# A fourth profile of widths for the experts, and a hand-ordered opening and end for the attention between them

## The chip, the cores and the metric

The program runs on one core of a Trainium2 chip. The metric is the time of one execution in microseconds (us); the median of the three runs before is 4838.47 us (4837.74 to 4840.27). The core has a matrix engine (TensorE, PE in the profile, with its weight loads apart as PEld), VectorE (DVE), ScalarE (ACT), GpSimd (POOL) and SyncE (SP), which issues most of the DMAs. PSUM, where PE leaves its results, has eight banks of 512 f32 numbers for each of 128 partitions.

## What is computed

A block of a transformer on x, 8 batches of 1024 rows of 512 numbers, all in f32:

```
x = x + 0.5 * ffn(layernorm(x))      # mixture of 32 experts, one for each row
x = x + attention(layernorm(x))      # 16 heads of 32, rope, softmax over 1024 keys
x = x + 0.5 * ffn(layernorm(x))      # the same ffn weights again

def ffn(xt):                         # xt: 8192 rows
    probs  = softmax(xt @ w_router)
    top1   = argmax(probs);  gate = probs[top1]
    pos    = place of the row among the rows of its expert
    accepted = pos < C               # C = ceil(1.25 * 8192 / 32) = 320
    y      = (silu(buf @ w_gate) * (buf @ w_up)) @ w_down     # for each expert, its rows in buf
    return xt + where(accepted, y * gate, 0)
```

The ffn adds its own (normalised) input as well. How many rows an expert gets depends on the data: the reference's routing of the given inputs sends between 191 and 343 rows to an expert in the first ffn, and between 160 and 429 in the second.

## The kernel before

Four stages follow each other in one program: the router of the first ffn (`Block.front`), its experts (`Block.experts`), the attention (`Attention.run`), which also does the router of the second ffn on its way, and the experts of the second ffn.

**Experts.** `Block.sorted` ranks the 32 experts by their number of rows. `Block.experts` then holds one program for each entry of `profiles` (L67): entry i gives a width for every rank, and the first entry whose widths hold all the experts' rows (the more-than-width flags are counted on VectorE, L478 to L481) is run through a switch. An expert of width w is given w columns: 64 MATMUL records of w columns against 128x128 weights for gate and up (`gated`, L704; each f32 product is two records), then for each block of 128 rows the down product (`feed`, L745, and L753 for the third block, which only widths over 256 have), with the transposes of the next expert's rows between (L692). Weights come by DMA two experts ahead.

**Attention.** A unit (b, c) is four heads of one batch. `stage` (L886) runs 16 slots over a unit: the score products for the row maxima and sums of one unit ("tops": L1220 on PE, L1235 on VectorE, L1239 on ScalarE), the score products, exponentials and weighted sums of the unit before ("sums": L1200, L1227, L1232, L1302), and between them one group of other PE work out of `fill`: projections of q and k for the unit after (`project`, L1125), of v (L1170), or the output product of the batch before (`output`, L1328). Small tasks (`prepare`: rows of the next batch loaded, normalised, transposed; `rotated`: rope on a projection; `finished`: router and routing of finished rows) are generators that `step` and `product` advance by due times and a credit of VectorE time. On PE, ScalarE, VectorE and GpSimd the order in which the program is written is kept; the DMA issues of SP are ordered by the framework. A projection's rope takes eight small DMAs (L1147, L1148), a product on GpSimd (L1150) and two on VectorE (L1153, L1154); all projections, transposes and output products use one PSUM bank, tag "m".

**The opening.** `constants` (L1006) loads tables and biases, then the output weights, and works out the output bias (bv times Wo, plus bo) with four products (L1040), split into three bf16 pieces. `run` (L921) then loads the v weights, prepares the first half of batch 0 and the second half after it (rows loaded, measured, normalised and evicted on VectorE), loads the q and k weights, and runs the four projections q, k, k, q of unit (0, 0); then the first stage starts.

**The end.** After the last unit, a stage of sums alone has the four output products of the last batch's first half in its slots 9 to 12; the four of the second half follow with VectorE adding each to the rows loaded from `x1` and storing to `x2`. `finished` then takes the first half (rows read back from `x2`, the rest of the row put out, normalised, transposed, router, routing), and after that the second half in the same way; `ranked` ranks the experts, and the table of rows is written to HBM for the second `experts`.

Of the kernel before, what the change touches and what calls it, by code (L numbers as in the profile page):

```python
# [50 lines left out]
class Block:  # L51


    def __init__(self, nc, tc, T, D, E, F):
# [11 lines left out]
        C, q = self.C, P // 4  # L66
        self.profiles = [  # L67
            [C] * 10 + [C - q] * 9 + [C - 2 * q] * 8 + [C - 3 * q] * (E - 27),
# [131 lines left out]
    def logits(self, hs, lg, pool, psum, tag, bufs=2):  # L200
# [4 lines left out]
        for h in hs:  # L205
            if isinstance(h, tuple):
                yield h
                continue
            yield PE, 0.6
            self.transposed(psum, tag, xT[:, :, j * P : (j + 1) * P], h)  # L210
            j += 1
# [558 lines left out]
class Attention:  # L770
# [13 lines left out]
    def __init__(  # L784
# [15 lines left out]
        self.credit = 0.0  # L800
        self.hT, self.w_qk, self.qk, self.v, self.oT = ({} for _ in range(5))
        self.mrow, self.over, self.mv, self.held = ({} for _ in range(4))
# [110 lines left out]
    def run(self):  # L913
        nc, tc = self.nc, self.tc
        F, KD = mybir.EngineType, self.KD
        with (
# [6 lines left out]
            with tc.manual_schedule(engines={F.PE, F.Activation, F.DVE, F.Pool}):  # L923
                self.s.copy = nc.vector.tensor_copy
                self.load(2)
                for half in range(2):
                    self.start(self.prepare(0, half, 0))
                    self.finish()
                self.load_qk(0, 0)
                for f in self.project(0, 0):  # L930
                    at_once(f())
                    self.now += 1
                    self.step(100)
                self.finish()
                units = [(b, c) for b in range(self.B) for c in range(KD)]
                for i, (b, c) in enumerate(units):
                    self.stage(
                        (b, c), units[i - 1] if i else None, self.fill(b, c), self.begin(b, c),
                        whole=(i == 0),
                    )  # L940
# [6 lines left out]
                for f in self.output(b, 1):  # L947
                    at_once(f())
                    self.now += 1
                    self.step(100)  # L950
# [24 lines left out]
    def fill(self, b, c):  # L975

        qk = self.project(*self.following(b, c))
        if b == c == 0:
            self.v_groups = self.values(0)
            v, self.v_groups = self.v_groups[:7], self.v_groups[7:]  # L980
            return dict(enumerate(qk + v))
# [24 lines left out]
    def constants(self, wp):  # L1006
        nc, s, KD, L = self.nc, self.s, self.KD, self.L
        D = s.D
        bq, bk, bv, bo = self.biases

        self.cs, self.sn = (a.rearrange("p k c -> p (k c)")[:, 0:L] for a in s.acts)
        nc.sync.dma_start(self.cs, self.cos)
        nc.sync.dma_start(self.sn, self.sin)
# [18 lines left out]

        bo_ = self.pool.tile([P, D], F32, tag="oT", bufs=9, name="bo")
        nc.sync.dma_start(bo_, bo.partition_broadcast(P))
        self.load(3)
        pb = self.psum.tile([P, D], F32, tag="m", name="pb")
        for k in range(KD):
            wide = self.pool.tile([P, P], F32, tag="wide", name="wide")
            nc.vector.tensor_copy(wide, self.bias[:, 2, k : k + 1].to_broadcast([P, P]))
            nc.tensor.matmul(  # L1040
                pb, wide, self.w_vo[:, k, :], start=(k == 0), stop=(k == KD - 1)
            )
        nc.vector.tensor_tensor(bo_, bo_, pb, ALU.add)

        self.bo16 = wp.tile([P, D], BF16, name="bo16")
        nc.vector.memset(self.bo16, 0.0)
        piece = self.pool.tile([P, D], BF16, tag="piece", bufs=1, name="piece")
        for i in range(3):
            nc.vector.tensor_copy(piece, bo_)
            p = slice(i * 32, i * 32 + 1)  # L1050
            nc.vector.tensor_copy(self.bo16[p, :], piece[p, :])
            nc.vector.tensor_tensor(bo_, bo_, piece, ALU.subtract)

# [6 lines left out]
    def loaded(self, which):  # L1060

        self.load(which)
        yield from ()
# [3 lines left out]
    def prepare(self, b, half, later):  # L1067
# [26 lines left out]
        self.there.add((b, half))  # L1094

# [216 lines left out]
    def output(self, b, half):  # L1312
        nc, pool, KD, D = self.nc, self.pool, self.KD, self.s.D
        work = []
        for j in range(4):

            def group(j=j):
# [3 lines left out]
                x = pool.tile([P, D], F32, tag="xr", name="xr")  # L1321
                nc.sync.dma_start(x, self.x1[t * P : (t + 1) * P, :])
                acc = self.psum.tile([P, D], F32, tag="m", name="px")
# [23 lines left out]
    def finished(self, b, half, counted=None):  # L1347

        nc, s, pool, D = self.nc, self.s, self.pool, self.s.D
# [148 lines left out]
```

## Time and profile before

| | us |
|---|---|
| median of 3 runs | 4838.47 |
| the profiled execution: its time | 4848.97 |
| its span, first to last instruction | 4847.2 |
| first expert product of stage 1 to its last | 186.39 to 964.94 |
| first expert product of stage 2 to its last | 4057.87 to 4836.04 |
| first score product of the attention | 1032.54 |
| last weighted sum of the attention | 3962.9 |

All times below are from the start of the span. A line of a timeline has the start, the duration, the engine, the line of the code, the operation, what it writes and reads, the shapes and how many records are merged (x8); in brackets, how long the engine was idle before and who released it. In the table by stretches, each engine has its busy time and its records; PEclk is the share of full clock that was granted to PE, and the DMA share is the mean over 16 engines. The chain is followed backwards from the last instruction, each step to what released it.

### The profile page before, as it was taken

What the parts mean: (1) busy time and instruction counts of PE and PEld (TensorE: products, weight loads), DVE (VectorE), ACT (ScalarE), POOL (GpSimd) and SP (SyncE); (2) the same over time, 40 slices, a digit from 0 to 9 for tenths busy, and PEclk for the clock granted to TensorE, in tenths of its full rate; (3) what the DMA queues carried; (4) which work ended last, traced back from release to release, by engine and by line L of the source; (5) the groups of instructions that cost most, each with busy time, mean ns of one, the idle gap of its engine ahead of it and who ended that gap; (6) DMA issues with size and microseconds to landing.
All of it is one profiled execution on the core that took longest, in us unless ns stands there. A gap on an engine that the chain in (4) does not pass through costs nothing.

```text
span 4847.2 us, 68820 instructions
## 1 busy us (share of the span) xinstructions
PE 4596.5 (95%) x24572; PEld 2128.0 (44%) x24572; DVE 2836.3 (59%) x5568; ACT 2923.5 (60%) x5856; POOL 790.4 (16%) x787
## 2 busy tenths in 40 slices
PE   6699999968999999999999999999999886999999
PEld 4466667722233333333333333333333234666677
DVE  8433333356666767767777767767767744333332
ACT  6221212128998888888888888888888841111111
POOL 4433333210000010110110110110110002222221
PEclk8799999979999999999999999999999997999999
DMA  4455566521111212212212212212212124455554
GB/s 142 148 187 184 190 197 220 178 85 29 34 30 60 75 38 65 70 42 65 70 42 65 70 42 65 69 42 66 60 43 57 49 70 154 158 174 177 171 193 137
DMA packets 290581, 486.02 MB, mean 100 GB/s; under 512 B 47895, under 2 KB 83169, under 8 KB 290224
## 3 DMA queue, kind: packets, MB, share of 16 engines
q1 hardware_dynamic: 255376, 404.36, 26.8%
q0 software_dynamic: 34560, 76.93, 5.2%
q8 instruction: 196, 3.21, 0.3%
q14 instruction: 161, 1.32, 0.1%
q10 hardware_dynamic: 288, 0.20, 0.0%
HBM read 380.11 MB, written 89.72 MB: 97 GB/s over the span
## 4 chain that ended last, share of the span: by engine, by line
PE 82%; DVE 7%; ACT 4%; issue 3%; DMA 2%; POOL 1%; SPq 1%; another core or an unknown queue 0%; DVEq 0%; POOLq 0%; ACTq 0%
PE sa L1220 13%; PE gp L704 10%; PE up L704 9%; PE pq L1125 9%; PE po L1302 9%; PE yp L745 9%; PE sb L1200 6%; PE px L1328 4%; PE pv L1170 4%; PE sb L1227 3%; ACT junk L1239 2%; DVE nm L1235 2%; PE tp L194 2%; DMA table<-row,slot 1%; PE yp L753 1%
## 5 line engine op out<-in xcount | busy, mean ns | idle before, releaser
L1235 DVE TENSOR_REDUCE nm<-sa 128x2 f32<-128x1024 f32 x1024 | 1248.7, 1220 | 648.3 <-PE sa L1220 386.9
L1239 ACT ACTIVATE junk<-sa,nm 128x512 f32<-128x512 f32 x2048 | 1407.3, 687 | 257.6 <-DVE nm L1235 177.0
L1220 PE MATMUL sa<-k,q 32*128 32x512 f32 x4096 | 1149.1, 645 | 17.9 <-ACT junk L1239 11.1
L1232 ACT ACTIVATE pr<-sb 128x1024 f32<-128x1024 f32 x1024 | 1040.5, 1018 | 101.3 <-PE sb L1227 97.4
L1227 PE MATMUL sb<-q,k 32*128 32x512 f32 x4096 | 1062.1, 602 | 0.0
L709 ACT ACTIVATE sg<-gp 128x320 f32<-128x320 f32 (+3 forms) x256 | 102.6, 401 | 1166.2 <-PE gp L704 1164.2
L1150 POOL TENSOR_TENSOR raw<-raw,a 128x512 f32<-128x512 f32 x128 | 164.2, 1283 | 2401.7 <-DMA rot<-raw 1645.0
L1302 PE MATMUL po<-pr,v 128*32 128x512 f32 x4096 | 548.0, 606 | 0.1
L704 PE MATMUL gp<-bT,wg 128*128 128x320 f32 (+3 forms) x2048 | 530.7, 402 | 0.0
L704 PE MATMUL up<-bT,wu 128*128 128x320 f32 (+3 forms) x2048 | 524.8, 399 | 0.0
L1125 PE MATMUL pq<-hT,wqk 128*128 128x512 f32 x1024 | 511.3, 624 | 4.9 <-DVE raw L1140 3.9
L745 PE MATMUL yp<-wd,a 128*128 128x512 f32 x1024 | 460.3, 592 | 0.0
L704 PEld LDWEIGHTS gp<-bT,wg 128*128 128x128 f32 x2048 | 386.7, 190 | 115.7 <-issue 26.7
L1200 PE MATMUL sb<-mrow,ones 3*128 3x512 bf16 x2048 | 392.9, 384 | 42.0 <-ACT pr L1232 40.7
L728 DVE TENSOR_TENSOR a<-sg,up 128x320 f32<-128x320 f32 (+3 forms) x256 | 114.0, 445 | 541.6 <-PE up L704 371.1
L704 PEld LDWEIGHTS up<-bT,wu 128*128 128x128 f32 x2048 | 388.9, 190 | 94.1
L1200 PEld LDWEIGHTS <-ones 3*128 3x128 bf16 x2048 | 99.6, 91 | 709.6 <-issue 670.1
L1239 ACT ACTIVATION_READ_ACCUMULATOR junk<-sa,nm 128x1 f32 x2048 | 398.2, 194 | 0.0
L1227 PEld LDWEIGHTS sb<-q,k 32*128 32x128 f32 x4096 | 359.7, 184 | 0.1
L1220 PEld LDWEIGHTS sa<-k,q 32*128 32x128 f32 x4096 | 304.9, 184 | 81.3 <-ACT pr L1232 30.3
L1125 PEld LDWEIGHTS pq<-hT,wqk 128*128 128x128 f32 x1024 | 176.2, 191 | 323.8 <-issue 227.0
L749 DVE SCALAR_TENSOR_TENSOR ys<-yp,gates,x 128x512 f32<-128x512 f32 x128 | 96.1, 751 | 336.8 <-PE yp L745 336.8
(178 smaller groups left out, 4241.8 us busy)
## 6 DMA issues: line engine op xcount, KB each, us to landing
wg<-in_w_gate SPq DMA_DIRECT2D x64, 1024.0 KB
wu<-in_w_up SPq DMA_DIRECT2D x64, 1024.0 KB
wd<-in_w_down SPq DMA_DIRECT2D x64, 1024.0 KB
rot<-raw SPq DMA_DIRECT2D x1024, 32.0 KB
all<-in_x SPq DMA_DIRECT2D x32, 512.0 KB
xt<-first_rows SPq DMA_DIRECT2D x64, 256.0 KB
xr<-first_rows SPq DMA_DIRECT2D x64, 256.0 KB
d<-inverse SPq DMA_DIRECT2D x256, 64.0 KB
```

Of the source, the lines that this page charges most:

```text
L704: nc.tensor.matmul(acc, w[:, k, f * P : (f + 1) * P], to.bT[:, k, 0:width], start=(k == 0), stop=(k == s.KD - 1),)
L745: nc.tensor.matmul(yp, a[:, f, i * P : (i + 1) * P], wd[:, f, :], start=(f == 0), stop=(f == KF - 1),)
L1125: nc.tensor.matmul(acc, w[:, which, k, :], self.hT[b, n][:, k, :], start=(k == 0), stop=(k == KD - 1),)
L1170: nc.tensor.matmul(acc, hT[:, k, at : at + P], self.w_vo[:, k, :], start=(k == 0), stop=(k == KD - 1),)
L1200: nc.tensor.matmul(sb[:, h, :], self.ones16[at : at + 3, :], row[at : at + 3, :], start=True, stop=False,)
L1220: nc.tensor.matmul(sa[:, h, :], qa[at, (g * 4 + j) * P : (g * 4 + j + 1) * P], ka[at, m * 512 : (m + 1) * 512], start=True, stop=True,)
L1227: nc.tensor.matmul(sb[:, h, :], k[at, t * P : (t + 1) * P], q[at, n * 512 : (n + 1) * 512], start=False, stop=True,)
L1232: nc.scalar.activation(pr, sb, AF.Exp)
L1235: nc.vector.tensor_reduce(nm[:, m, j, pair : pair + 2], sa, AX.X, ALU.max, negate=True)
L1239: nc.scalar.activation(self.junk, sa[:, h - pair, :], AF.Exp, bias=nm[:, m, j, h : h + 1], accum_out=se[:, m, j, h : h + 1],)
L1302: nc.tensor.matmul(self.po[at : at + HD, :], self.v[b][t][:, c * P + at : c * P + at + HD], prs[h // 2 * 2][:, h % 2, :], start=(t == 0), ...
L1328: nc.tensor.matmul(acc, self.oT[b, c, half][:, j * P : (j + 1) * P], self.w_vo[:, c, :], start=False, stop=(c == KD - 1),)
```

## The change

- `profiles` gets a fourth entry, put first, with widths in steps of 16: 6 experts of 320, 1 of 304, 5 of 288, 6 of 272, 3 of 256, 5 of 240, 3 of 224, 3 of 208. Entry 0 before (10 of 320, 9 of 288, 8 of 256, 5 of 224) becomes entry 1.
- A new `opening` takes the place of the prologue in `run`. The q and k weights are loaded first, then the first four row tiles, the rope tables, and the other four row tiles (each half with buffers of its own). Each row tile is measured by itself; ScalarE normalises; three PSUM tags (s0 to s2, those of the scores) take the transposes; VectorE evicts the first half, ScalarE the second. Only k and q of the first half are projected before the first stage, the second half's transposes stand behind them, and the other two projections become the first two fills of that stage, in front of the eleven that it has.
- The output bias is worked out later: in stage (1, 1), with the first load of the output weights, and on one partition.
- At the end, the rows of the last batch stay on chip: they are not read back from `x2`. The second half's output products have the tags s0 to s2, and between them two turns of the first half's router work. ScalarE normalises and evicts the transposes of both halves; the second half's transposes use s0, s1, s2 and "po". The second half's router waits for the first half's logits, and only the routing waits for the first half's routing. The rest of the second half's rows is put out after the routing.

```diff
-        C, q = self.C, P // 4
+        C, q, h = self.C, P // 4, P // 8
         self.profiles = [
+            [C] * 6 + [C - h] + [C - 2 * h] * 5 + [C - 3 * h] * 6 + [C - 4 * h] * 3
+            + [C - 5 * h] * 5 + [C - 6 * h] * 3 + [C - 7 * h] * (E - 29),
             [C] * 10 + [C - q] * 9 + [C - 2 * q] * 8 + [C - 3 * q] * (E - 27),
...
-                self.load(2)
-                for half in range(2):
-                    self.start(self.prepare(0, half, 0))
-                    self.finish()
-                self.load_qk(0, 0)
-                for f in self.project(0, 0):
-                    at_once(f())
-                    self.now += 1
-                    self.step(100)
-                self.finish()
+                later = self.opening()
...
                 for f in self.output(b, 1):
                     at_once(f())
                     self.now += 1
-                    self.step(100)
+                    for _ in range(2):
+                        self.step(100)
+                        self.product()
...
-            return dict(enumerate(qk + v))
+            return dict(enumerate(ahead + qk + v))
...
     def loaded(self, which):
         self.load(which)
-        yield from ()
+        if which == 3 and not self.biased:
+            self.biased = True
+            yield from self.output_bias()
+
+    def output_bias(self):
+        nc, pool, KD, D = self.nc, self.pool, self.KD, self.s.D
+        bo = pool.tile([P, D], F32, tag="xr", name="bo")[0:1, :]
+        nc.sync.dma_start(bo, self.biases[3].partition_broadcast(1))
+        yield WAIT, 2
+        yield PE, 3.4
+        pb = self.psum.tile([P, D], F32, tag="m", name="pb")[0:1, :]
+        for k in range(KD):
+            nc.tensor.matmul(
+                pb, self.bias[:, 2, k : k + 1], self.w_vo[:, k, :],
+                start=(k == 0), stop=(k == KD - 1),
+            )
+        nc.vector.tensor_tensor(bo, bo, pb, ALU.add)
+        piece = pool.tile([P, D], BF16, tag="piece", bufs=1, name="piece")[0:1, :]
+        for i in range(3):
+            nc.vector.tensor_copy(piece, bo)
+            nc.vector.tensor_copy(self.bo16[i * 32 : i * 32 + 1, :], piece)
+            if i < 2:
+                nc.vector.tensor_tensor(bo, bo, piece, ALU.subtract)
...
+    def opening(self):
+        self.load_qk(0, 0)
...
+        xs = [fetch(0)]
+        nc.sync.dma_start(self.cs, self.cos)
+        nc.sync.dma_start(self.sn, self.sin)
+        xs.append(fetch(1))
...
+        for j in range(4):
+            measure(0, j)
+        for j in range(4):
+            measure(1, j)
+            kept(0, j, turn(0, j))
+        at_once(steps[-1])
+        self.there |= {(0, 0), (0, 1)}
+        q0, k0, k1, q1 = self.project(0, 0)
+        for f in (k0, q0):
+            at_once(f())
+        for j in range(4):
+            kept(1, j, turn(1, j))
+            self.now += 1
+            self.step(100)
+        self.load(2)
+        while self.tasks:
+            self.now += 1
+            self.step(100)
+        return [k1, q1]
...
     def output(self, b, half):
...
+        last = b == self.B - 1
...
-                x = pool.tile([P, D], F32, tag="xr", name="xr")
+                tag, bufs = ("xt", 4) if last and not half else ("oT", 9) if last else ("xr", 2)
+                x = pool.tile([P, D], F32, tag=tag, bufs=bufs, name="xr")
+                kept.append(x)
-                acc = self.psum.tile([P, D], F32, tag="m", name="px")
+                acc = self.psum.tile(
+                    [P, D], F32, tag=f"s{j % 3}" if last and half else "m", name="px"
+                )
...
     def finished(self, b, half, counted=None):
...
+        def last_rows():
+            while self.weighted < half:
+                yield WAIT, 1
+            for j, x in enumerate(self.kept[half]):
+                h = pool.tile([P, D], F32, tag="h3", bufs=3, name="h3")
+                s.normalize(h, x, by, j)
+                if not half:
+                    put_kept(j)
+                yield h
...
+        yield from s.logits(
+            last_rows() if last else rows(), lg, pool, self.psum, "m", bufs=1,
+            tags=("s0", "s1", "s2", "po") if last and half else ("m",) * 4 if last else None,
+        )
+        self.weighted += last
+        while self.routed < b * 2 + half:
+            yield WAIT, 1
         self.carry = yield from s.route(
             first, lg, pool, self.psum, "m", self.carry, self.table, counted=counted
         )
         self.routed += 1
+        if last and half:
+            for j in range(4):
+                put_kept(j)
```

`measure` is statistics and scale of one row tile (VectorE, with the power on GpSimd), `turn` the normalising on ScalarE and four transposes on PE, `kept` the eviction, `put_kept` the rest of a row on ScalarE and its DMA to `out`.

## The prediction

> **What bounds the kernel now.** I read the table by stretches first, since the whole-span shares average over stages.
>
> ```profile
> core 0: us, PE busy (x) PEld busy (x) DVE busy (x) ACT busy (x) POOL busy (x), PEclk, DMA share, GB/s
> 186.00:965.00 779.00, 778.94 (x3187) 537.42 (x3185) 280.14 (x723) 156.72 (x275) 248.25 (x258) 1.00 0.59 195
> 965.00:1054.00 89.00, 46.84 (x108) 19.96 (x111) 37.30 (x79) 7.51 (x17) 10.96 (x8) 0.69 0.37 108
> 1116.00:3963.00 2847.00, 2794.09 (x17206) 924.25 (x17207) 2020.97 (x3342) 2510.29 (x5075) 239.65 (x205) 1.00 0.19 55
> 3963.00:4058.00 95.00, 38.68 (x131) 21.20 (x130) 40.39 (x135) 3.45 (x7) 14.84 (x18) 0.61 0.29 95
> 4058.00:4836.00 778.00, 778.00 (x3184) 537.01 (x3184) 279.72 (x721) 111.54 (x210) 185.00 (x193) 1.00 0.53 174
> ```
>
> In both expert stretches PE never rests: what leaves PE there leaves the time. The attention's middle is PE at 98%. Between lie two stretches, 89 and 95 us, in which the busiest engine is busy 53% and 43% of the time and PE's clock is reduced: those are chains of waits. Next the timeline of PE in two experts:
>
> ```profile
> 356.75 2.32 PE L704 MATMUL gp<-bT,wg 128*128 128x320 f32 x8
> 358.91 2.32 PE L704 MATMUL up<-bT,wu 128*128 128x320 f32 x8
> ...
> 907.62 1.68 PE L704 MATMUL up<-bT,wu 128*128 128x224 f32 x8
> 909.13 1.68 PE L704 MATMUL gp<-bT,wg 128*128 128x224 f32 x8
> ```
>
> Starts, not durations, give the pace: eight records take 2.16 us at 320 columns and 1.51 at 224, so 0.65/(8 x 96) = 0.84 ns a column and record; no constant worth naming. Last the chain of waits in the opening:
>
> ```profile
> 970.46 7.66 DMA wvo<-in_woT
> 978.25 6.47 PE pb L1040 x8
> ...
> 1009.94 6.00 PE pq L1125 x8
> 1015.96 0.76 DVE raw L1140
> ...
> 1042.28 1.14 DVE nm L1235
> ```
>
> The output bias's weights and products come first, rows are turned one by one (a row's transposes 1.10, its eviction 0.69, each waiting for the other), and the first row maximum waits for all four projections' ropes.
>
> **The change part by part.**
>
> *Widths.* The reference's routing fits the new entry 0 in both ffns (tightest: 222 rows for a width of 224 in the first, 267 for 272 in the second), and the trace shows the old entry 0 in both. The sum of widths falls from 8960 to 8560: 400 columns x 64 records x 0.84 ns = 21.4 us a stage. One expert, from 288 to 256 columns, loses its third block: 16 half-width products (615.06 to 616.94, 1.88 us) and four transposes, 0.44: 2.3. Weights stay covered: at 224 columns an expert takes 19.85 us with PE fully busy, and a gate weight is issued at 877.19 for use at 906.1; at 208 an expert still takes 19.0. Twice 23.7 is **-47.4**. One flag more is counted in each ffn (two operations, 0.15 each on VectorE): +0.3.
>
> Is there a floor under the width? At 224 columns the weight loads are busy without a gap, 1.51 us for eight (907.43), as long as the products. Were that their own pace, 208 columns would gain nothing: three experts x 16 columns, 2.6 us a stage. But at 32.63 eight loads of the same 128x128 f32 weights, for 32-column products, take 0.97 us, 0.12 each, under the 0.17 that 208 columns need. That row is nearer, since there the loads set the pace; I take no floor and keep 5.2 us for the range.
>
> A rule speaks against it. The Trainium skill, Perfetto Trace Analysis, "Identifying the Most-Contended Engine", calls matmul busy time a bad measure and has PE's headroom read from the busy share of its weight loads. By that rule the loads, gapless at 224 columns, would be full, and the widths would bring 42.2 in place of 47.4; the row at 32.63 decides against it.
>
> *Opening.* The instruction order of both programs is the same on PE, VectorE and ScalarE from the second unit to the last sums, but for the output bias; so what counts is when the first stage runs clear. Before, slot 2 of it begins at 1053.9. After, from 970.1, when the last scattered rows have landed as now:
> - q and k weights take 0.71 + 0.81 to issue, then come the rows. The first lands between 973.6 (issue plus the 1.95 that a small rope DMA takes) and 978.8 (as now, behind a 1 MB load): I take 975, since half a MB is ahead of it.
> - VectorE: eight rows measured, 1.4 each by the expert's opening row (4051.47 to 4052.82), and four evictions of 0.69: 13.9, to 989. ScalarE's normalising (0.82) and the transposes (1.10) run beside it on three PSUM tags.
> - k, 6.00 as at 1009.94 at half clock, its eviction 0.76, eight rope issues in 5.1 and 1.95 to land. q follows in 3.70, evicted at 1001; SP is free of k's issues by then, so q's rope lands at 1008.2, GpSimd 1.7, VectorE 0.7: 1010.6. Behind q, the second half needs 4 x 2.65 on PE and ScalarE (0.82 + 1.10 + 0.58 and hand-overs): 1011.2. The two agree on 1011 for slot 0.
> - Slots 0 and 1 with their projections: between 4.8 each (the later filled slots) and 7.5 (2.08 + 5.46 at half clock, 1046.42). I take 6.2, as the clock comes back in the middle: slot 2 at 1023.5, **30.4 earlier**.
> - Given back: fills reach two slots further, 4.9 for 3.5 us (slots 11 to 15, 1099.0 to 1116.5): 2.8; and eight rope issues, 5.1, are longer than a filled slot, for four slots: 1.2.
>
> That is **-26.4**, from -32 (rows early, short slots) to -18 (rows late 3.8, slots 2.6 longer, q at half clock 2.3). The batch-1 row loads, bo and xr that SP has ahead of the ropes wait for transposes that end by 987, and so block nothing.
>
> *Output bias.* Moved into stage (1, 1): eight records of 512 columns, 3.4 us on a PE that has no slack. Its DMA and the weights (issued at 1473.92 now, 15 us ahead) are in time. VectorE gets nine small operations, 4.2 us by 984.74 to 991.97 (0.7, 0.4, 0.3), with the next row maxima queued behind; VectorE is 71% busy there. Between 0 and 7.6, I take **+4**: PE's share and a little.
>
> *End.* Before, the second half's first transposes start at 4010.28 and its router product at 4021.15. After: first px to 3966.6; add, statistics and scale 1.8 to 3968.4; normalising 0.82; the first two rows turned by 3972.6 (ScalarE also puts out the rest, 0.8); px 3.75; two rows; px; router product; px to 3987.8; fold product to 3988.8; VectorE copies, maxima and counts 3.3 + 0.9 to 3992.9; prefix product and its read 1.1; scale to 3994.5. Then four rows at 2.65 (before 2.95): router product at 4005.2, **-16**. From there on the chain is the same; the rest's stores have some 15 us beside it. Ends: -20 (the interleaved rows cost PE nothing), -9 (one window at half clock 3.4, ScalarE waiting for a store 3.5).
>
> *Sum:* -47.4 + 0.3 - 26.4 + 4 - 16 = -85.5. The profiled execution took 4848.97, so 4763.5; the median of the runs lies 10.5 under it: **4753**. All low ends: 4739. All high ends, with the weight loads' 5.2: 4779.
>
> **The rivals.**
> 1. *The narrow widths don't run.* If rounding on the chip gives one expert three rows more, a stage falls back to the old widths: 23.7 back, 4777. Against it: rows change experts only in near ties. 4%.
> 2. *SP holds the opening.* SP issues in order, and at 986.17 its row loads took 23.33 us because they waited for transposes. If the batch-1 loads again wait behind late transposes, the ropes start some 10 us later: 4763. Against it: these four wait for the first half only. 12%.
> 3. *ScalarE holds the end.* What VectorE did is serial on ScalarE now, up to 2.2 us a row; if PE waits for it at each row, 12 us come back: 4765. 8%.
> 4. *Slower: the middle loses the clock.* PE has full clock from 1298 to 3984. If the shifted start left a gap in each of 31 stages that drops it to half for 6.8 us (the granted windows' length here), each loses 3.4: +105, 4858. It decides from 85.5/31 = 2.8 us a stage on. Against it: the order in those stages is unchanged. 3%.
>
> **How the numbers follow.** The forecast as it stands has 73%, its own range 4740 to 4772; with rivals 2 and 3 it fills the range 4737 to 4776, about 88% of the cases before errors in reading them. 0.2% (9.7 us) is what a measurement can tell here. Faster 95% (all but rival 4 and a little of the unforeseen), same 1%, slower 4%.
>
> **What would show it.** Experts at 208 columns 19.0 us apart, those at 320 still 27.48; PE without rest in both stages; gate and up starts 1.40 us apart for eight at 208. First row maximum near 1012 less 23.7, so about 988; slot 2 near 1000. Stage (1, 1) 3 to 5 us longer, the other stages at 90.6. From last weighted sum to first expert product 79 instead of 95 us. It is wrong if eight loads at 208 columns still take 1.51, if ropes wait on SP for rows, or if the middle stages change.

## The result, and the profile after

| | us |
|---|---|
| before, median of 4 runs | 4838.98 (4837.74 to 4840.27) |
| after, median of 4 runs | 4758.70 (4754.59 to 4760.98) |
| ratio after to before | 0.9831, 95% interval 0.9819 to 0.9842 |
| forecast | 4753, range 4737 to 4776 |

The changed kernel is 80.3 us faster; the forecast was 85.5, which lies inside the interval of the measurement (76 to 88 us). The profiled execution of after took 4757.85 us, close to its median, while that of before, at 4848.97, lay 10 above its own, so spans can't be compared as a whole. Both executions cut at the same events give this (an expert stage goes from its first gate product to its last down product; a unit begins with its first score product):

| stretch | before | after | difference | forecast |
|---|---|---|---|---|
| start to first expert product | 186.39 | 175.72 | -10.7 | the 10.5 above the median |
| experts, stage 1 | 778.55 | 754.17 | -24.4 | -23.7 |
| from there to the second unit | 151.6 | 121.1 | -30.5 | -26.4 |
| units (0, 1) to (1, 0) | 349.0 | 352.7 | +3.7 | (in the row above) |
| unit (1, 1), with the bias | 88.5 | 96.4 | +7.9 | +4 |
| units (1, 2) to the one before the last | 2266.1 | 2266.9 | +0.7 | 0 |
| last unit and its sums | 142.8 | 144.2 | +1.4 | 0 |
| last weighted sum to first expert product | 94.99 | 79.12 | -15.9 | -16, and +0.3 for the flag |
| experts, stage 2 | 778.17 | 754.96 | -23.2 | -23.7 |

Without the first row the differences sum to -80.3, and the last 10.8 us, after the experts, add -0.3: nearly what the medians say. Each row is one execution against one. Where other traces of this case have the same code in a stretch, they differ there too: the opening of after, to the second unit, took 121.1 to 125.4 us in six traces, its end 76.9 to 79.5 in six, the last unit 142.8 to 147.2 in all thirteen. So tenths in this table are readings of two executions, not of the edits. The table by stretches of the kernel after, its columns as before:

```profile
core 0: us, PE busy (x) PEld busy (x) DVE busy (x) ACT busy (x) POOL busy (x), PEclk, DMA share, GB/s
176.00:930.00 754.00, 753.89 (x3164) 532.76 (x3164) 275.47 (x717) 153.12 (x273) 245.84 (x255) 1.00 0.61 201
930.00:983.30 53.30, 27.64 (x84) 12.80 (x84) 23.67 (x69) 15.13 (x27) 9.46 (x12) 0.71 0.40 129
1051.00:3911.00 2860.00, 2803.03 (x17215) 926.41 (x17214) 2025.83 (x3350) 2510.80 (x5073) 239.04 (x205) 1.00 0.19 54
3911.00:3990.00 79.00, 37.44 (x132) 20.84 (x130) 26.55 (x111) 19.43 (x30) 14.42 (x18) 0.65 0.26 91
3990.00:4745.00 755.00, 755.00 (x3166) 533.49 (x3164) 275.99 (x717) 108.81 (x210) 183.23 (x191) 1.00 0.54 179
```

PE still never rests in the expert stretches, so all that the widths took from PE left the time. The second row is the opening up to slot 2, 53 us in place of 89. At the end PE does nearly the work that it did before (37.4 us, 38.7 before): what went is waiting. In the opening PE's busy time fell as well, from 46.8 to 27.6, since the output bias and two projections now stand behind it; the other 16.5 us are waiting that went. Gate and up products of an expert at the narrowest width, in the timeline of PE:

```profile
911.60 1.57 PE L712 MATMUL gp<-bT,wg 128*128 128x208 f32 x8
913.01 1.57 PE L712 MATMUL up<-bT,wu 128*128 128x208 f32 x8
914.42 0.52 PE L712 MATMUL gp<-bT,wg 128*128 128x208 f32 x2
```

Starts are 1.41 apart (forecast 1.40), and an expert of 208 columns takes 19.00 us (forecast 19.0), one of 320 still 27.48. The chain that ended last, in the opening of after:

```profile
935.18 4.27 DMA xt<-first_rows
939.58 0.71 DVE st L153
...
951.30 0.61 DVE hT L1149
951.95 5.23 PE pq L1200 x8
957.20 0.76 DVE raw L1215
957.98 0.63 SPq L1222
...
966.86 0.59 SPq L1222
967.49 1.94 DMA rot<-raw
969.68 1.80 POOL raw L1225
971.50 0.70 DVE q L1229
972.34 2.09 PE sa L1295 x8
```

The rows come first now, VectorE's work on them has no hole until 951.9, then come k's projection, sixteen DMA issues one after the other on SP, their starts 0.63 apart, and q's rope. No wait for output weights is left, and the first score product follows the last expert product by 42.5 us (67.6 before).

### The profile page after: what moved, and what is told of

It reads as the page before. It is cut to its first block, busy times and chain, and to the rows that moved or that the text cites. A ratio compares the mean times of both kernels' runs of the same rounds, so it can differ in the third digit from the quotient of the medians.

```text
span 4756.0 us, 68742 instructions
## 1 busy us (share of the span) xinstructions
PE 4538.9 (95%) x24532; PEld 2114.6 (44%) x24532; DVE 2811.0 (59%) x5542; ACT 2942.7 (62%) x5890; POOL 788.9 (17%) x798
## 4 chain that ended last, share of the span: by engine, by line
PE 82%; DVE 7%; ACT 4%; issue 3%; DMA 2%; POOL 1%; SPq 1%; DVEq 0%; POOLq 0%; ACTq 0%
PE sa L1295 13%; PE gp L712 9%; PE up L712 9%; PE pq L1200 9%; PE po L1377 9%; PE yp L753 9%; PE sb L1275 6%; PE px L1411 4%; PE pv L1245 4%; PE sb L1302 3%; ACT junk L1314 2%; DVE nm L1310 2%; PE yp L761 1%; PE tp L700 1%; PE tp L196 1%
## 5 line engine op out<-in xcount | busy, mean ns | idle before, releaser
L717 ACT ACTIVATE sg<-gp 128x320 f32<-128x320 f32 (+7 forms) x256 | 99.6, 389 | 1122.1 <-PE gp L712 1120.9
L712 PE MATMUL gp<-bT,wg 128*128 128x272 f32 (+7 forms) x2048 | 509.2, 392 | 0.0
L712 PE MATMUL up<-bT,wu 128*128 128x272 f32 (+7 forms) x2048 | 503.5, 389 | 0.0
L736 DVE TENSOR_TENSOR a<-sg,up 128x320 f32<-128x320 f32 (+7 forms) x256 | 110.7, 433 | 506.5 <-PE up L712 368.9
L1295 PEld LDWEIGHTS sa<-k,q 32*128 32x128 f32 x4096 | 303.2, 183 | 70.7 <-ACT pr L1307 30.4
```

The source lines that it names most:

```text
L712: nc.tensor.matmul(acc, w[:, k, f * P : (f + 1) * P], to.bT[:, k, 0:width], start=(k == 0), stop=(k == s.KD - 1),)
L1295: nc.tensor.matmul(sa[:, h, :], qa[at, (g * 4 + j) * P : (g * 4 + j + 1) * P], ka[at, m * 512 : (m + 1) * 512], start=True, stop=True,)
```

## The experiments

All times are medians of four runs, against the kernel before on the same chip in the same comparison:

| kernel | us | before there | difference | ratio, 95% interval |
|---|---|---|---|---|
| after | 4758.70 | 4838.98 | -80.3 | 0.9819 to 0.9842 |
| a1_widths | 4789.47 | 4839.63 | -50.2 | 0.9876 to 0.9909 |
| a2_old_opening | 4780.83 | 4839.63 | -58.8 | 0.9865 to 0.9898 |
| a3_bias_last | 4765.12 | 4839.63 | -74.5 | 0.9829 to 0.9861 |
| a4_old_end | 4773.92 | 4839.63 | -65.7 | 0.9849 to 0.9882 |
| b1_no_bias | 4773.62 | 4840.51 | -66.9 | 0.9843 to 0.9876 |
| b2_four_ahead | 4770.96 | 4840.51 | -69.6 | 0.9839 to 0.9872 |
| b3_end | 4752.82 | 4840.51 | -87.7 | 0.9804 to 0.9837 |
| b4_bias_open | 4753.17 | 4840.51 | -87.3 | 0.9816 (0.98 to 0.9832) |
| c1_best | 4755.36 | 4849.78 | -94.4 | 0.9788 to 0.9821 |
| c2_best_narrow | 4731.82 | 4849.78 | -118.0 | 0.9741 to 0.9774 |

The last comparison ran on a chip where every kernel was some 10 us slower, the kernel before too; there the differences count, not the times. An interval of these ratios is 11 to 16 us wide, so a difference of a few us between two rows is no more than a sign; below it is always set beside the stretches of the traces. b5_floor stands apart: it leaves out rows and ran once.

### a1_widths: the new widths alone

```diff
 # on the kernel before
+            [C] * 6 + [C - h] + [C - 2 * h] * 5 + [C - 3 * h] * 6 + [C - 4 * h] * 3
+            + [C - 5 * h] * 5 + [C - 6 * h] * 3 + [C - 7 * h] * (E - 29),
             [C] * 10 + [C - q] * 9 + [C - 2 * q] * 8 + [C - 3 * q] * (E - 27),
```

> The kernel before with the new entry of widths alone; opening, output bias and end as before. My account (0.84 ns a column and record, one third block less a stage): each expert stage 778.4 becomes 754.2 to 755.0 as in the changed kernel, so 47.6 us less than before and 0.3 more for the third flag: 4791 to 4792. Rival, the widths' gain depends on the other edits (earlier weights at the second stage, for instance): then the second stage alone stays above 757 and the time above 4794. Rival, weight loads set the pace at 208 columns: 4796.

Measured: expert stages of 755.05 and 755.43 us, 46.2 less than before; the attention as before, 1.5 longer; time 50.2 less, with 60 to 44 inside its interval. The widths are worth nearly what the columns say (46.2 where 47.6 was expected), and need neither of the other edits. The first account holds; the two rivals, 757 or more in the second stage and a floor, don't.

### a2_old_opening: the bias out of the opening, but the old order

```diff
 # on the changed kernel
-                later = self.opening()
+                self.load(2)
+                for half in range(2):
+                    self.start(self.prepare(0, half, 0))
+                    self.finish()
+                self.load_qk(0, 0)
+                for f in self.project(0, 0):
+                    at_once(f())
+                    self.now += 1
+                    self.step(100)
+                self.finish()
+                later = []
...                                       # the rope tables are loaded in constants again
+        nc.sync.dma_start(self.cs, self.cos)
+        nc.sync.dma_start(self.sn, self.sin)
```

> The changed kernel with the opening as it was (v weights first, rows normalised and evicted on VectorE one after the other, four projections ahead of the first stage), but with the output bias still in stage (1, 1). It tells what of the opening's 27.7 us comes from taking the bias's weights and products out of it, and what from the hand-made order. Account A, the order: rows still land behind 1 MB of v weights and their chain of 2.42 us each stays, so taking the bias out brings only the interleaved pieces, 2 us or so: some 25 us slower than the changed kernel, 4783 to 4785. Account B, the bias: the weights' 7.66 us and the products' 6.47 stood in the path, so 12 to 14 us of the gain stay without the new order: 4771 to 4773.

Measured: the second unit starts 149.2 us after the last expert product (151.6 before, 121.1 after), and the time is 21.5 us worse than the changed kernel's, by the differences to before. So taking the bias's megabyte and products out of the opening gave 2.4 us, and the order 28.1, of which 22.0 are left at the end of the attention (3082.4 against 3060.3). Even the 2.4 may be chance: a1, whose opening still has the bias, reached its second unit after 148.7 us. Account A holds, with 21.5 us where it said some 25. In the chain before, the 7.66 us of the output weights and the 6.47 of the products look like 14 us of path; behind them stood a second chain, the rows one by one, that was about as long. A step on the chain is worth only its distance to the next chain.

### b2_four_ahead: all four projections before the first stage

```diff
 # on the changed kernel, at the end of opening
+        for f in (k1, q1):
+            at_once(f())
+            self.now += 1
+            self.step(100)
         self.load(2)
...
-        return [k1, q1]
+        return []
```

> The changed kernel with the other two projections of unit (0, 0) run ahead of the first stage again instead of as its first two fills; rows, engines and PSUM tiles of the new opening are kept. Account A: VectorE takes its work in order, so the first row maximum again stands behind the ropes of all four projections; it moves from 44.6 us after the last expert product to 57 or so, the second stage 7 to 10 us later, and of that 2 to 3 come back because the fills end two slots earlier: 5 to 7 us slower than the changed kernel, 4764 to 4766. Account B: most of the opening's gain is in rows and engines, the ropes run beside the score products: 0 to 2 us, 4759 to 4761.

Measured: the first row maximum 62.7 us after the last expert product in place of 44.6, the second unit 13.9 us later, the time 10.7 worse. VectorE's timeline in this kernel:

```profile
985.64 0.69 DVE L1232 TENSOR_TENSOR rot<-rot,a 128x512 f32<-128x512 f32 x1 [2.66 <-DMA rot<-raw]
987.48 0.69 DVE L1233 TENSOR_TENSOR k<-raw,rot 128x512 f32<-128x512 f32 x1 [1.16 <-POOL raw L1229]
990.90 0.69 DVE L1232 TENSOR_TENSOR rot<-rot,a 128x512 f32<-128x512 f32 x1 [2.73 <-DMA rot<-raw]
992.75 0.69 DVE L1233 TENSOR_TENSOR q<-raw,rot 128x512 f32<-128x512 f32 x1 [1.15 <-POOL raw L1229]
993.36 1.22 DVE L1314 TENSOR_REDUCE nm<-sa 128x2 f32<-128x1024 f32 x1
```

The score products were there (PE began them at 982.12), but the maximum is queued behind two ropes that each wait for a small DMA. The mechanism is that of account A, and larger than it said, since the first of the two late projections also ran at half clock (6.78 us). Of the opening's gain some 11 us are this one decision; the other half of a2's difference goes with the rest of the order (loads, engines, PSUM tags), which no run takes apart.

### b1_no_bias: what the output bias costs

```diff
 # on the changed kernel
         if which == 3 and not self.biased:
             self.biased = True
-            yield from self.output_bias()
+            yield from ()
```

> The changed kernel without the work on the output bias (its four products and nine VectorE operations are left out, so the output lacks that bias). Account: stage (1, 1) is 96.4 us with it and 88.5 in the kernel before; all of the 7.9 us is the bias: 88.5 again, 7.9 us under the changed kernel, about 4750.8. Rival: part of it belongs to the shifted order of stage 1 and stays: 2 to 4 us of gain only.

Measured: stage (1, 1) 88.5 us, the attention 8.0 us shorter at the start of the last unit: all of the 7.9 us comes with the bias. But the whole is slower than the changed kernel. Without the bias the second ffn's router gets other numbers; its rows no longer fit the new widths, and the second stage runs the old entry (ten experts at 320 columns, then 288):

```profile
core 0: us, PE busy (x) PEld busy (x) DVE busy (x) ACT busy (x) POOL busy (x), PEclk, DMA share, GB/s
3981.50:4760.30 778.80, 778.77 (x3185) 537.50 (x3184) 279.99 (x721) 111.79 (x211) 185.30 (x193) 1.00 0.52 174
```

778.8 us against 755.0 is the price of rival 1 of the forecast: 23.8 (23.7 was forecast). It also shows how near the widths are fitted to one set of inputs.

### a3_bias_last: the product that reads the bias at the end of its group

```diff
 # on the changed kernel, in output
-                nc.tensor.matmul(acc, self.ones16, self.bo16, start=True, stop=False)
                 for c in range(KD):
...
-                        start=False, stop=(c == KD - 1),
+                        start=(c == 0), stop=False,
                     )
+                nc.tensor.matmul(acc, self.ones16, self.bo16, start=False, stop=True)
```

In the changed kernel the timelines of PE, VectorE and ScalarE in stage (1, 1) show what the bias holds up:

```profile
1435.85 3.60 PE L1057 MATMUL pb<-wvo,bias 128*1 128x512 f32 x8
1439.48 0.68 DVE L1061 TENSOR_TENSOR bo<-bo,pb 1x512 f32<-1x512 f32 x1 [3.09 <-PE pb L1057]
...
1443.46 0.28 DVE L1065 COPY bo<-piece 1x512 bf16<-1x512 bf16 x1
...
1443.81 0.61 PE L1407 MATMUL px<-bo,ones 128*128 128x512 bf16 x1 [3.18 <-DVE bo L1065]
...
1446.12 0.69 ACT L1314 ACTIVATE junk<-sa,nm 128x512 f32<-128x512 f32 x1 [4.42 <-DVE nm L1310]
```

> The changed kernel with the product that adds the output bias put last in each output group instead of first. In the changed kernel stage (1, 1) takes 96.4 us against 88.5 before; the first output group starts 3.2 us late, waiting for the last of the nine VectorE operations on the bias. Account A: that wait is about half of the 7.9 us; with the bias product two slots later it is gone: stage (1, 1) 92 to 93, time 3.5 to 4.4 us under the changed kernel, about 4754.5. Account B: VectorE's queue is what delays the stage (row maxima stand behind the nine operations, ScalarE idles 4.4 us for them), so the wait only moves to the score products: 0 to 1 us.

Measured: stage (1, 1) 98.2 us, longer still, and the time 5.8 worse than the changed kernel's. In a3 the first output product runs at 1441.01 without waiting, and this stands in the next slot:

```profile
1446.55 0.69 ACT L1314 ACTIVATE junk<-sa,nm 128x512 f32<-128x512 f32 x1 [4.39 <-DVE nm L1310]
...
1448.19 0.61 PE L1275 MATMUL sb<-mrow,ones 3*128 3x512 bf16 x2 [3.02 <-ACT junk L1314]
1449.11 1.22 PE L1295 MATMUL sa<-k,q 32*128 32x512 f32 x2 [0.31 <-ACT pr L1307]
```

The wait of 3.18 has become one of 3.02 of the score products for ScalarE, which waits for the row maxima, which stand behind the nine operations: account B. After it PE's clock is at half for 6.8 us (score products 1.22 in place of 0.70), where the changed kernel has 3.4 us of it. That can be the whole of the 1.8 us by which this stage is longer: b2 and b3, which have the changed kernel's code here, also had 6.8 us at half clock, and took 97.9 and 97.8. Account A, and with it the first reading of that wait, falls: the wait that a profile names can be removed and the time stay, when the same queue delays something else next. Most of the 5.8 us is elsewhere: later stages with output groups were mostly 0.2 to 0.5 us longer, 4.9 over all. Slots with the second half of a group, where the moved product now stands, mostly took 0.21 more, and those with the first half 0.12 less or the same. Why the sum isn't zero stays open.

### b4_bias_open: the bias where PE and VectorE wait anyway

```diff
 # on the changed kernel, in opening
+        wo = [pool.tile([P, s.D], F32, tag="oT", bufs=9, name="wo") for _ in range(self.KD)]
+        for k, t in enumerate(wo):
+            nc.sync.dma_start(t, self.weights[3][k * P : (k + 1) * P, :])
...
             kept(1, j, turn(1, j))
+            nc.tensor.matmul(
+                pb, self.bias[:, 2, j : j + 1], wo[j], start=(j == 0), stop=(j == 3)
+            )
...
+        nc.vector.tensor_tensor(bo, bo, pb, ALU.add)
+        self.start(self.bias_pieces(bo), rank=3)
...                                       # bias_pieces has the splitting; loaded has no bias work
```

> The changed kernel with the output bias in the opening: the output weights go into four free tiles behind the other loads (no transfer runs from 952 to 958), the four products stand between the second half's transposes, where PE waits 1.4 us for ScalarE each time, the sum is taken when VectorE is idle, and the pieces run as a small task in the first stage. Account: stage (1, 1) back to 88.5, the first stage at most 1 us longer: 6 to 8 us under the changed kernel, 4751 to 4753. Rival: the products or the megabyte of weights hold the second half's rows or ropes, and the opening gives 3 us or more back: 4755 or more.

Measured: stage (1, 1) 88.5, the first score product at 43.0 (42.5), the first stage 2.2 longer, attention 5.9 shorter in all, time 7.0 less than the changed kernel's by the differences to before. The account holds in the time, with more given back than the 1 us it allowed: the second unit starts 2.8 later, just under the 3 of the rival. The pieces still pass through VectorE in the first stage; whether they are what holds it isn't shown, and the same opening without them varies as much.

### a4_old_end and b3_end: the end undone, and the end taken further

```diff
 # a4_old_end, on the changed kernel
-                    for _ in range(2):
-                        self.step(100)
-                        self.product()
+                    self.step(100)
...
-                tag, bufs = ("xt", 4) if last and not half else ("oT", 9) if last else ("xr", 2)
+                tag, bufs = "xr", 2
...
-                    [P, D], F32, tag=f"s{j % 3}" if last and half else "m", name="px"
+                    [P, D], F32, tag="m", name="px"
...
-        last = b == self.B - 1
+        last = False                      # in finished
```

> The changed kernel with the end as it was: rows read back from HBM, the PSUM tag m alone, no router work between the output products, VectorE for normalising and evicting. Account: last weighted sum to first expert product 95 us again in place of 79.1, and the last stage 1.4 us shorter: 17 us slower than the changed kernel, 4773 without the 1.4 and 4776 with it. Rival: part of the 15.9 us comes from the shifted clock windows rather than from the edit; then 8 us or so, 4767.

Measured: last weighted sum to first expert product 94.5 us (79.1 after, 95.0 before), time 14.6 worse than the changed kernel's. So 15.4 of the 15.9 us go with the edit, and the account holds; its 17 us came as 14.6. The last unit with its sums was 143.5, between before and after, so the 1.4 us there are not shown to be part of the edit. The shifted clock windows are not what brought the gain.

In the changed kernel's end, VectorE has the second half's statistics at 3938.97, but its scale comes after the first half's routing, and each row then waits for the one before:

```profile
3938.79 0.18 DVE L154 BATCH_NORM_AGGREGATE mv<-st 128x2 f32<-128x6 f32 x1
...
3942.01 0.17 DVE L164 TENSOR_SCALAR rstd<-mv 128x4 f32<-128x4 f32 x1
...
3944.42 1.12 PE L196 MATMUL tp<-ident,h 128*128 128x128 f32 x4 [1.71 <-ACT h L174]
3946.98 1.12 PE L196 MATMUL tp<-ident,h 128*128 128x128 f32 x4 [1.44 <-ACT h L174]
3949.48 1.11 PE L196 MATMUL tp<-ident,h 128*128 128x128 f32 x4 [1.39 <-ACT h L174]
```

```diff
 # b3_end, on the changed kernel
-                self.start(self.finished(b, 1, self.ranked))
+                self.start(self.finished(b, 1, self.ranked), rank=1)
...
+        if last and half:
+            by = at_once(s.normalizing(pool, self.mv[b, half]))
...
-            while self.weighted < half:
-                yield WAIT, 1
-            for j, x in enumerate(self.kept[half]):
-                h = pool.tile([P, D], F32, tag="h3", bufs=3, name="h3")
-                s.normalize(h, x, by, j)
-                if not half:
-                    put_kept(j)
-                yield h
+            ahead(0)                      # normalises one row
+            for j in range(4):
+                ahead(j + 1)
+                yield hs[j]
+                if not half:
+                    put_kept(j)
```

> The changed kernel with another order at the end: the second half's scale is worked out before the first half's routing, its four transposes stand before the routing's prefix product, and in both halves a row is normalised ahead of the eviction of the row before. In the changed kernel the second half's scale waits 3.1 us behind the routing's maxima and counts on VectorE, its four rows take 2.55 us each because ScalarE and PE wait for each other, and PE waits 1.4 us twice in the first half's rows. Account: 3 + 3.4 + 2.5 us less, with a little lost to the routing that is now later: last weighted sum to first expert product from 79.1 to 71 to 73, time 4751 to 4753. Rival: the routing of the first half, now behind, holds the second half's: 0 to 3 us of gain.

Measured: 72.5 us from last sum to first expert product, 6.6 less; time 7.4 less than the changed kernel's by the differences to before. PE's timeline in b3:

```profile
3942.82 1.38 PE L196 MATMUL tp<-ident,h 128*128 128x128 f32 x8 [3.36 <-ACT h L174]
3944.92 2.30 PE L196 MATMUL tp<-ident,h 128*128 128x128 f32 x8 [0.72 <-ACT h L174]
3947.89 1.93 PE L231 MATMUL pl<-xT,w_router 128*32 128x512 f32 x8 [0.68 <-ACT xT L214]
```

The four rows take 5.1 us from the first transpose to the router product in place of 9.35 (3944.42 to 3953.77). The account holds: 72.5 lies in its 71 to 73, and of the 8.9 us that it listed, 6.6 arrived. Counted from the first output product the router product comes 8.3 us earlier than in the changed kernel; 1.7 of that are lost behind it. The rival, that the postponed routing takes nearly all of it back, does not hold.

### b5_floor: how far the pace follows the columns

```diff
 # on the changed kernel: one entry, for whatever rows there are
-            + [C - 5 * h] * 5 + [C - 6 * h] * 3 + [C - 7 * h] * (E - 29),
+            + [C - 5 * h] * 5 + [208, 192, 176, 160, 144, 136],
```

> The changed kernel with its last six experts held to 208, 192, 176, 160, 144 and 136 columns whatever their rows (the rows above are left out; it is a look at the pace alone). Account, pace by columns without a floor: eight gate records start 1.40, 1.29, 1.18, 1.08, 0.97 and 0.91 us apart, an expert loses 0.86 us for each step of 16 columns, 18.1 at 192 and 15.5 at 144. Rival, weight loads set a floor near the width where they are gapless: the starts stay at 1.3 to 1.4 from 192 on and the experts at 18 us or more. A third, weights from HBM: three MB for each expert can't come in less than some 16 us, then PE rests between the last experts but the eight records still keep the pace.

Measured: experts of 208 to 144 columns took 19.00, 18.14, 17.29, 16.44 and 15.59 us, 0.85 to 0.86 for each sixteen columns, and PE had no rest between them. The last expert in the timelines of PE and of the weight loads:

```profile
909.54 1.09 PE L709 MATMUL gp<-bT,wg 128*128 128x136 f32 x8
910.47 1.09 PE L709 MATMUL up<-bT,wu 128*128 128x136 f32 x8
...
911.28 1.00 PEld L709 LDWEIGHTS gp<-bT,wg 128*128 128x128 f32 x8
912.21 1.00 PEld L709 LDWEIGHTS up<-bT,wu 128*128 128x128 f32 x8
```

Eight records start 0.93 us apart at 136 columns (0.91 expected), and eight weight loads, still without a gap, take 1.00. A weight load's record stretches to the pace of the products: busy without a gap at 224 columns, it was not the limit there, nor anywhere down to 136. The Trainium skill, Perfetto Trace Analysis, "Identifying the Most-Contended Engine", would have PE's headroom read from the share of peak arithmetic and the busy share of these loads; of the second, for these f32 products, the traces disagree, since loads that looked full at 224 columns went on to 0.93 us for eight. No floor showed; where one begins is below 136 columns and open. The weights' DMA didn't show either: three MB in 16 us is the mean rate of the expert stage before (195 GB/s), and here 282 GB/s were moved from 878 to 894.5 while PE never rested. But no weights follow a stage's last expert, so six narrow ones at its end are no test of a lasting rate.

### c1_best and c2_best_narrow: what the experiments point to

c1 is b3 and b4 together; c2 has in addition widths in steps of 8:

```diff
 # c2_best_narrow, on c1
+            [C] * 4 + [C - e] + [C - 2 * e] * 2 + [C - 4 * e] + [C - 5 * e] * 4 + [C - 6 * e] * 2
+            + [C - 7 * e] * 3 + [C - 8 * e] + [C - 9 * e] * 2 + [C - 10 * e] * 4
+            + [C - 11 * e] * 2 + [C - 12 * e] * 3 + [C - 14 * e] + [C - 15 * e] * 2,
```

with e = 8, in place of the entry in sixteens.

> Both: the changed kernel with the output bias in the opening and the end in its new order. The two touch different stretches, so the gains should add: 5.8 us (first stage and stage (1, 1)) and 6.6 us (last weighted sum to first expert product, 72.5 in place of 79.1), 4746 to 4747. Rival: the last stage, 2 us longer when the end alone was reordered (146.1 for 144.2), is longer through the new order and not through the clock windows that fall in it; then 4748 to 4749.

> The same with the first entry of widths in steps of 8 columns in place of 16, each again at least two above the rows of the reference's routing: sum 8400 for 8560, and one expert more without a third block. At 0.84 ns a column and record 160 columns are 8.6 us a stage, the block 2.3: expert stages 743.3 and 744.1 for 754.2 and 755.0, 21.8 us less in all, 4724 to 4726. Rival: an odd number of eights costs a column more than the sixteens do (other evictions, other transposes), or the rows miss the narrower widths in one ffn; then 4736 to 4747.

Measured, by the traces: c1's attention takes 3048.0 us from the last expert product of stage 1 to the first of stage 2, 12.3 less than the changed kernel's 3060.3 (12.4 was expected): the gains add, although the last unit took 147.2. The old end can have a last unit nearly as long, 146.1 in a1 (see the last section), so it needn't be the new order; that the new order has no part in it isn't shown, as b3 and c2 were long there too (146.2 each). c2's expert stages take 743.6 and 743.3, 22.8 us less than c1's 755.0 and 754.7; 21.8 was expected. Against before, c1 is 94.4 us faster and c2 118.0, a ratio of 0.9757: it beats both kernels, if for these inputs; widths of eights leave fewer rows to spare, and b1 shows what a miss costs.

## Why the prediction was right

- *Widths*, -47.4 and +0.3: measured -47.6 in the stages. Right, and for the reason given: starts, not durations, set the pace, and nothing else was bound up with them (a1, -46.2). (400 x 64 x 0.84 ns is 21.5, not 21.4.) Taking the row at 32.63 against the gapless loads was the right choice (b5).
- *Opening*, -26.4: -30.5 at the second unit, -27.6 at the third, -26.8 at unit (1, 1). Right in sum by two errors that nearly cancel, which is luck. Slot 2 moved 35.5 us earlier, not 30.4: slot 0 began 42.5 us after the last expert product, not 46.1 (VectorE was through its rows at 22.0 for a forecast 24.1, and k took 5.2 instead of 6.0), and slots 0 and 1 took 5.5 each instead of 6.2. Given back by the third unit were 7.9 (5.0 in the first unit, 2.9 in the next), not 4.0. The 2.9 goes with the clock, which the forecast did not count there: the same code took 87.7 us in that unit in before, 88.9 in b3 and 90.5 in after, with 3.9, 6.8 and 9.9 us of it at half clock.
- *Output bias*, +4 in 0 to 7.6: measured +7.9. This is the step that failed. The forecast let VectorE's nine operations run beside PE, "PE's share and a little". They stand on the path (a3, b1): products 3.60, then 4.3 from the sum to the last copy. That the two add up to 7.9 is in part chance, since the stage also has 3.4 us of half clock (1443.1 to 1446.6, none there in before), and took 9.3 and 9.4 more than before where it had 6.8; how much of the 7.9 is clock isn't shown. Two things had not been seen: the first output group comes in the very next slot and begins with the product that reads the pieces, and even where it doesn't (a3), the row maxima queue behind the pieces and hold the score products.
- *End*, -16: measured -15.9. The second half's router product was forecast 42.4 us after the first output product and came 42.7 after it. Rows at 2.5 each against 2.65 forecast. The path is right (a4); the agreement to a tenth is luck, since the same end took 76.9 to 79.5 us in other traces and the old one 94.5 to 95.2.
- *Left out*: 0.7 us in the middle units and 1.4 in the last one, not costed at all. Both are within what traces of the same code differ by there.
- *The profiled execution's 10.5 above the median* was taken off, and rightly so: it is in the router's stage ahead of the experts, which no edit touches.

Of the rivals, the widths ran (rival 1; its price was right, b1). SP did not hold the opening: its row loads for batch 1 took 4.04 us from 943.89, where 23.33 were spent on row loads before, and the ropes found SP free (rival 2). ScalarE did hold the rows at the end by 1.4 us each (rival 3), but that was inside the 2.65 that the forecast paid for a row; b3 shows that 6.6 us were to be had there. The middle kept its clock (rival 4): 1.00 in the mean from 1051 to 3911, and full without a break from 1446.6 to 3839.3.

The sum missed by 5.2 us: 3.9 for the bias, 2.1 for what was left out, less 0.8 by which widths, opening and end did better. The range was a little wide by a slip: its high ends add up to 4777, not 4779.

## What to carry to other kernels

Cut two traces at the same events before comparing anything: here a 10 us difference of one execution lay wholly outside the edit, and every term could then be read by itself. Then look at the same stretch in every trace that has the same code there: here they differed by 2.6 to 4.4 us in the opening, the end and the last unit, and a term can't be read more finely than that. A wait on the chain is worth its distance to the next chain, and a queue that causes one wait can have a second one ready: move the work off the queue (b4), not the waiter (a3). When work moves into a stage that is full, add the engines' shares that follow each other unless a slot between them is seen to be free.

## What the runs showed of the hardware that was not expected

The last unit and its sums, the same instructions in all kernels but for the tiles named (and, in a3, the place of the bias product), took 142.8 to 147.2 us. Before and a1, which have the same code there, in the table by stretches:

```profile
core 0: us, PE busy (x) PEld busy (x) DVE busy (x) ACT busy (x) POOL busy (x), PEclk, DMA share, GB/s
3820.10:3962.90 142.80, 123.33 (x894) 41.17 (x894) 75.24 (x162) 111.33 (x201) 9.92 (x10) 1.00 0.14 44
```

```profile
core 0: us, PE busy (x) PEld busy (x) DVE busy (x) ACT busy (x) POOL busy (x), PEclk, DMA share, GB/s
3784.40:3930.50 146.10, 127.10 (x894) 41.88 (x894) 75.27 (x162) 112.28 (x201) 9.93 (x10) 0.96 0.14 43
```

The granted clock differs, 1.00 and 0.96: it falls to half in windows of 3.4 us, none in before, three in a1. Over all thirteen traces: no window 142.8; one 143.5 to 144.2; two 145.1 to 146.2; three 146.1 to 147.2. So each window goes with 0.7 to 1.7 us, and after, 1.4 longer than before, has one. What calls a window in one execution and not in another stays open. The Trainium skill, TensorE: Matmul & The Clock Gate, "Part 1: The HAM clock gate", has PE at full clock after one busy window of about 3.4 us; the lengths here, 3.4, 6.8 and 10.2, agree with such a unit. In b4, where the bias products filled PE's pauses between the opening's transposes, the later three fours of these took 0.66 us each, where after's later two took 1.1.

The router's stage at the very start, the same in all, ended at 175.4 to 176.6 us in nine profiled executions and at 185.1 to 186.5 in four: that of before, and all three kernels of the last comparison. VectorE in after and in c1 at the same instruction:

```profile
138.46 0.29 DVE L313 TENSOR_TENSOR lg<-pp,oh 128x128 f32<-128x128 f32 x1 [0.66 <-PE pp L307]
```

```profile
149.70 0.29 DVE L313 TENSOR_TENSOR lg<-pp,oh 128x128 f32<-128x128 f32 x1 [6.42 <-remote]
```

In c1 VectorE stands for 6.4 us although PE had its product done at 143.9; the trace names no engine or transfer. It is 10 us, more than most steps of this change, and its cause is open.
